# The last row of the first sweep ends in two halves of 256 columns

## The chip, the cores and the metric

The kernel runs on one core of a Trainium2 chip. The metric is the device time of one execution in microseconds. Three runs of the kernel before took 1407.41, 1408.8 and 1412.98 us; their median is 1408.8 us. The profile comes from a further execution that took 1410.98 us and whose span, from the first to the last instruction, is 1409.2 us.

## What is computed

Four graph layers follow one another over N = 4096 nodes with 64 features and one adjacency matrix `adj` of 4096 x 4096 (64 MB in f32). Each layer's result is added to its input and layer-normalised. Only the first layer matters here, a Chebyshev filter with four weights:

```
def layer0(x, L, weight):                 # L = adj, K = 4
    terms = [x, L @ x]
    for _ in range(2, K):
        terms.append(2.0 * (L @ terms[-1]) - terms[-2])
    return einsum('kni,kio->no', stack(terms), weight)
x = layernorm(x + layer0(x, adj, L0_weight))
```

The kernel works it backwards, so that features and weights are multiplied first. With w0 to w3 the four weights, b3 = x w3, b2 = x w2 + 2 A b3, b1 = x w1 + 2 A b2 - b3, and the layer gives x w0 + A b1 - b2. Three products with the whole matrix follow one another, and each needs the one before.

## The kernel before, in words

**Tiles.** The 4096 rows are 8 groups (`NG`) of 512 rows, the columns 8 groups of 512. A tile is 512 rows by 512 columns, 1 MB. `cheb_n` holds for each of 32 blocks of 128 nodes three slots of 64 features: slot 0 is b3, slot 1 becomes b2, slot 2 becomes b1. `nat_a` collects the layer's result.

**The first sweep** (the loop over `g` near line 640) loads every tile of `adj` as it stands (`raw`, SyncE's DMA queue), row group after row group, the columns from the last to the first. A tile is turned by 16 TensorE transposes (L657) into four PSUM tiles `tp`, which ScalarE copies to the turned tile `at` (L664). The turned tile is written back to memory (`adj_t`, GpSimd's queue, L686) for all that follows. VectorE takes a row sum and a minimum from the raw tile (L688, L690, 2.3 us each). The products of a tile are put one tile late: `tile_before`, the function of the previous tile, is called after the transposes of the current one. A tile at or right of the diagonal is multiplied by `halves` (L559): 64 feature columns of weights, blocks of even and odd number into the two halves of the partitions of `h_ps`. A tile left of the diagonal is multiplied by `both` (L566): slots 0 and 1 of `cheb_n` together, 128 weight columns, so that `w_ps` holds A b3 in partitions 0 to 63 and A b2 in 64 to 127 (b2 of the lower row groups is there by then).

**The end of a row** is `after_first`. VectorE adds the A b3 part of `w_ps` to `t_h`, the copied `h_ps` (L604), and ScalarE copies its A b2 part to `t_w` (L605). Then come four steps. `first` turns `t_h` back to rows and adds it twice into slot 1, which is b2 of this row (L580 or L585, then L588). `on_diagonal` multiplies the diagonal tile by that b2 into `d_ps` (L559) and adds `t_w` (L614). `second` does for slot 2 what `first` did for slot 1. `taken_off` subtracts b2 from `nat_a` on GpSimd (L622). In rows 0 to 6 these steps lie one by one between the tiles of the next row. In the last row, g = 7, nothing is left to put between, and they follow one another.

`twice_into` has two ways. Rows up to 4 use pair products: `t` is the weight and `pair`, two identity matrices of 64 stacked, the moving operand, which turns the block and adds its two halves in one product (L585). Rows 5 to 7 use transposes (L580) and two additions of 64 features each (L588, twice).

**The second sweep** goes through the tiles right of the diagonal, from row group 6 down. Its first tile is (6, 7), whose weights are slots 1 and 2 of the *last* row group (`both`, L566, target `pass`). VectorE makes the tile's mask (L754, 1.2 us) and GpSimd's queue stores it (L497). The tiles come from `adj_t` through SyncE's queue (L712), each into a buffer that a matmul or a mask of an older tile has to free first. The third sweep (L559, `pass`) follows in the same manner, and then the other layers.

**Order.** Operations recorded through `in_order` keep their program order on their engine; the others are placed by a scheduler. PSUM has eight banks: three `tp`, two `post`, and one each for `h_ps`, `w_ps` and `d_ps` (the pool `ps_a`). The targets of the second sweep use the banks of `h_ps` and `w_ps` in turn.

Of the kernel before, what the change touches and what calls it, by code (L numbers as in the profile page):

```python
# [9 lines left out]
F32 = mybir.dt.float32  # L10
# [5 lines left out]
ALU = mybir.AluOpType  # L16
# [46 lines left out]
def gnn4_kernel(  # L63
# [21 lines left out]
    nc = tc.nc  # L85
    P = 128
    N, F = x.shape
    NB = N // P
    GB = 4
    GW = GB * P  # L90
    NG = NB // GB
    CB = 4
# [26 lines left out]
    def load_raw(g, c):  # L119
        raw = row_tile("raw")  # L120
        nc.sync.dma_start(raw, adj[gcols(g), c * CB * P : (c + 1) * CB * P].rearrange("(b p) j -> p b j", p=P))
        return raw
# [19 lines left out]
    pair = const.tile([P, F], F32, name="pair")  # L142
# [25 lines left out]
    nat_a = keep.tile([P, NB, F], F32, name="nat_a")  # L168
# [36 lines left out]
    def in_order(ins):  # L205
        return tc.keep_in_program_order(ins)

    def cols(b):
        return slice(b * P, (b + 1) * P)

    def gblocks(g):
        return slice(g * GB, (g + 1) * GB)
# [312 lines left out]
    with tc.tile_pool(name="acc", bufs=1) as acc_p, tc.tile_pool(  # L525
        name="cols0", bufs=4
    ) as cols_p, tc.tile_pool(name="kept0", bufs=1) as kept_p, tc.tile_pool(name="diag0", bufs=2) as diag_p, tc.tile_pool(
        name="ps_t0", bufs=3, space=PSUM
    ) as ps_t, tc.tile_pool(name="ps_a0", bufs=1, space=PSUM) as ps_a, tc.tile_pool(
        name="ps_p0", bufs=2, space=PSUM  # L530
    ) as ps_p:

        cheb_n = acc_p.tile([P, NB, 3, F], F32, name="cheb_n")

        t_w = [acc_p.tile([P, GW], F32, name=f"t_w{q}") for q in range(2)]
# [20 lines left out]
        def halves(ps, k, rhs, jb, first, last):  # L556

            q = jb % 2
            in_order(nc.tensor.matmul(  # L559
                ps[q * F : (q + 1) * F, :], lhsT=cheb_n[:, jb, k, :], rhs=rhs,  # L560
                start=first, stop=last, skip_group_check=True,
            ))

        def both(ps, k, rhs, jb, first, last):

            in_order(nc.tensor.matmul(ps, lhsT=cheb_n[:, jb, k : k + 2, :], rhs=rhs, start=first, stop=last))  # L566

        def out_of(ps, name):
            t = acc_p.tile([P, GW], F32, name=name, tag=name if name == "t_h" else "tcol", bufs=2)
            nc.scalar.copy(t, ps)  # L570
            return t

        def new_post(w=F):
            return ps_p.tile([P, GB, w], F32, name="post", tag="post")
# [23 lines left out]
        def after_first(g, t_h, w_ps, diag_at):  # L598

            gs = gblocks(g)  # L600
            d_ps = ps_a.tile([P, GW], F32, name="d_ps")
            t_d = acc_p.tile([P, GW], F32, name="t_d", tag="tcol", bufs=2)
            if g:
                in_order(nc.vector.tensor_tensor(t_h[0:F, :], w_ps[0:F, :], t_h[0:F, :], ALU.add))  # L604
                nc.scalar.copy(t_w[g % 2][F:P, :], w_ps[F:P, :])  # L605

            def first():
                twice_into(cheb_n[:, gs, 1, :], t_h, g)

            def on_diagonal():  # L610
                for k in range(CB):
                    halves(d_ps, 1, diag_at[:, k, :], g * GB + k, k < 2, k >= 2)
                if g:
                    in_order(nc.vector.tensor_tensor(t_d, d_ps, t_w[g % 2], ALU.add))  # L614
                else:
                    nc.scalar.copy(t_d, d_ps)

            def second():
                twice_into(cheb_n[:, gs, 2, :], t_d, g)

            def taken_off():
                nc.gpsimd.tensor_tensor(nat_a[:, gs, :], nat_a[:, gs, :], cheb_n[:, gs, 1, :], ALU.subtract)  # L622

            return [first, on_diagonal, second, taken_off]


        win = ExitStack()
        win_p = win.enter_context(tc.tile_pool(name="win", bufs=1, side="right"))
        loads, weight_steps = attention_weights(win_p, ps_p)
# [6 lines left out]
        while weight_steps:  # L636
            row, c = divmod(len(aside), NCH)
# [5 lines left out]
        for g in range(NG):  # L643
            h_ps = ps_a.tile([P, GW], F32, name="h_ps")
            w_ps = ps_a.tile([P, GW], F32, name="w_ps") if g else None
            row = {}
            for c in reversed(range(NCH)):
                raw = first_raw.pop() if first_raw else load_raw(g, c)
                if g == NG - 1 and 4 <= c < g:
                    at = kept_p.tile([P, CB, GW], F32, name="at", tag="at") if c == g - 1 else before[:, c - 4]  # L650
                else:
                    at = (diag_p if c == g else cols_p).tile([P, CB, GW], F32, name="at", tag="at")
                for k in range(CB):
                    jb = c * CB + k
                    tp = ps_t.tile([P, GW], F32, name="tp", tag="tp")
                    for b in range(GB):
                        in_order(nc.tensor.transpose(tp[:, cols(b)], raw[:, b, cols(k)], ident))  # L657
                        if g * GB + b == jb:
                            scrap = sm.tile([P, P], F32, name="scrap")
                            in_order(nc.vector.scalar_tensor_tensor(  # L660
                                scrap, raw[:, b, cols(k)], 1.0, ident, ALU.mult, ALU.mult,
                                accum_out=diag[:, jb : jb + 1],
                            ))
                    nc.scalar.copy(at[:, k, :], tp)  # L664
                if steps0:
                    steps0.pop(0)()
                if tile_before:
                    tile_before()

                def tile_before(h_ps=h_ps, w_ps=w_ps, c=c, at=at, g=g, row=row):  # L670
                    for k in range(CB):
                        jb = c * CB + k
                        if c < g:
                            both(w_ps, 0, at[:, k, :], jb, c == g - 1 and k == 0, c == 0 and k == CB - 1)
                        else:
                            halves(h_ps, 0, at[:, k, :], jb, c == NCH - 1 and k < 2, c == g and k >= CB - 2)
                    if c == g:
                        row["at"] = at
                        row["t_h"] = out_of(h_ps, "t_h")
                    if c == 0:  # L680
                        steps0.extend(after_first(g, row["t_h"], w_ps, row["at"]))

                if aside:
                    for work in aside.pop(0):
                        work()
                nc.gpsimd.dma_start(adj_t[g][:, c * CB : (c + 1) * CB, :], at)  # L686

                in_order(nc.vector.tensor_reduce(dpart[:, g, c, :], raw, AX.X, ALU.add))  # L688
                n = g * NCH + c
                in_order(nc.vector.tensor_reduce(lows[:, n : n + 1], raw.rearrange("p b j -> p (b j)"), AX.X, ALU.min))  # L690
                if g == NG - 1 or (g == NG - 2 and c == g):
                    here[g, c] = at
        tile_before()
        for step in steps0:
            step()
# [12 lines left out]
        def load0(g, c, free=None):  # L708
            if (g, c) in here:
                return here[g, c]  # L710
            at = free.tile([P, CB, GW], F32, name="at", tag="at" if free in (cols_p, kept_p) else "raw") if free else row_tile("at")
            nc.sync.dma_start(at, adj_t[g][:, c * CB : (c + 1) * CB, :])  # L712
            return at
# [31 lines left out]
        for g in reversed(range(NG - 1)):  # L745
            ps = ps_a.tile([P, GW], F32, name="pass2", tag=("h_ps", "w_ps")[g % 2])
            for c in reversed(range(g + 1, NCH)):
                at = load0(g, c)
# [16 lines left out]
        due, n = [], 0  # L765
        for m, g in enumerate(third_rows):
            ps = ps_a.tile([P, GW], F32, name="pass3", tag=("h_ps", "w_ps")[m % 2])
            row = list(reversed(range(g + 1)))
            if m == 0:
                row = row[4:] + row[1:4] + row[:1]  # L770
            for c in row:
                at = load0(g, c, None if (g, c) in here else third_pools.pop(0))
# [408 lines left out]
    for signed in (False, True):  # L1181
        with cmp.Else() if signed else tc.If(all_positive > 0) as block:
            cmp = block
            with tc.tile_pool(name="cols1", bufs=3 if not signed else 2) as cols_p, tc.tile_pool(name="sign1", bufs=1) as sg, tc.tile_pool(
                name="tail1", bufs=1
            ) as tl, tc.tile_pool(name="ps_a1", bufs=1, space=PSUM) as ps_a, tc.tile_pool(
                name="ps_p1", bufs=2, space=PSUM
# [141 lines left out]
    with tc.tile_pool(name="mask2", bufs=3) as mk_p, tc.tile_pool(name="wt2", bufs=3) as wt_p, tc.tile_pool(  # L1329
        name="ps_c2", bufs=1, space=PSUM  # L1330
# [30 lines left out]
        for turn, groups in enumerate(turns_of):  # L1361
# [9 lines left out]
            for h in reversed(range(2 * NB)):  # L1371
                jb, odd = divmod(h, 2)
                c, k = divmod(jb, CB)
# [4 lines left out]
                for a in range(2):  # L1378
                    for r in range(2):
                        in_order(nc.tensor.matmul(  # L1380
                            cnt[a][r * HP : (r + 1) * HP, :], lhsT=follow, rhs=chunks[c][odd][2 * a + r][:, k, :],
                            start=(h == 2 * NB - 1), stop=True, skip_group_check=True,
# [7 lines left out]
                if odd:  # L1390
                    if turn == 0 and jb == NB - 1:
# [3 lines left out]
                        ps_a = ps_a_open.enter_context(tc.tile_pool(name="ps_a2", bufs=1, space=PSUM))  # L1395
                        acc = [ps_a.tile([P, GW], F32, name=f"acc_ps{q}") for q in range(QG)]
                    continue
                two = [
                    lambda half=half, a=a, jb=jb, wt=wt, acc=acc: gather_two(jb, half, a, wt, acc)
                    for half in (1, 0) for a in range(2)  # L1400
                ]
# [37 lines left out]
    with tc.tile_pool(name="o3", bufs=1) as op, tc.tile_pool(name="cols3", bufs=3) as cols_p, tc.tile_pool(  # L1439
        name="w3", bufs=4  # L1440
    ) as wp3, tc.tile_pool(name="el3", bufs=3) as el, tc.tile_pool(name="f3", bufs=2) as fp, tc.tile_pool(
        name="r3", bufs=2
    ) as rp, tc.tile_pool(name="ps_v3", bufs=2, space=PSUM) as ps_v, tc.tile_pool(
        name="ps_a3", bufs=2, space=PSUM
# [273 lines left out]
        n = 0  # L1718
        while n < NU + 2 or turns or gathers:
# [5 lines left out]
            if n < NU:  # L1725
                if n % 2 == 0:
                    fs[n // 2] = fp.tile([P, CB, GW], F32, name="f3")
                w, cs = ws[n][:, :, columns(n)], columns(n)
# [6 lines left out]
            if n >= 2 and n - 2 < NU:  # L1735
                m = n - 2
                t, h = divmod(m, 2)
                cm = columns(m)
                hs = slice(h * HB, (h + 1) * HB)
                f, at = fs[t][:, hs, cm], own[t][:, hs, cm]  # L1740
# [4 lines left out]
                diagonal = tiles[t][0] == tiles[t][1]  # L1745
# [82 lines left out]
```

## Time and profile before

| what | value |
|---|---|
| runs | 1407.41, 1408.8, 1412.98 us |
| the profiled execution | 1410.98 us, span 1409.2 us |
| TensorE busy | 1308.8 us (93%) |
| VectorE busy | 1051.4 us (75%) |
| ScalarE busy | 805.0 us (57%) |
| GpSimd busy | 109.9 us (8%) |
| memory traffic | 294 MB read, 85 MB written |
| last raw tile's transposes end | about 348.4 us |
| first product of the second sweep | 363.14 us |

Times inside the profile are microseconds from the span's start. TensorE's matmuls are recorded in passes: an f32 product is two records, a transpose is one. Records overlap: 512 columns start every 0.43 us and are marked 0.592 us long, so pitches are read from starts. PE is TensorE's matmul row, PEld its weight loads, DVE VectorE, ACT ScalarE, POOL GpSimd and SP SyncE; "granted clock" is the share of TensorE's full clock that it was given.

### The profile page before, as it was taken

The numbers are of one execution on the slowest core, as the hardware profiler recorded it, in microseconds if no ns is written. First come the engines' busy times: TensorE is split into PE (matmuls) and PEld (weight loads), VectorE is DVE, ScalarE is ACT, GpSimd is POOL, SyncE is SP. The second block draws the span as 40 slices with busy tenths as digits, with TensorE's granted clock in tenths as the row PEclk, the third lists the DMA queues.
The fourth block names the chain that finished last, engine by engine and source line by source line (L and its number), as shares of the span: only waits on it lengthen the run. The fifth ranks groups of instructions, "written<-read, shape, count | busy, mean of one in ns | idle before, by whom it ended". The sixth has DMA issues, their size and how long they took to land.

```text
span 1409.2 us, 18984 instructions
## 1 busy us (share of the span) xinstructions
PE 1308.8 (93%) x6766; PEld 605.2 (43%) x6766; DVE 1051.4 (75%) x2010; ACT 805.0 (57%) x1341; POOL 109.9 (8%) x191
## 2 busy tenths in 40 slices
PE   7999999999899999999999999997888898999883
PEld 5655555565344334444444323333333333333331
DVE  6699998999334257787885224356999999999996
ACT  4554444343000115654424675745989999999893
POOL 2111111101122000010111000000000000000000
PEclk9999999999999999999999999998999999999997
DMA  9999999999699999999985755534235353445320
GB/s 316 404 395 391 402 411 410 410 403 392 231 380 372 389 415 372 422 358 338 329 306 185 229 178 165 181 120 180 99 141 211 147 214 150 183 162 200 141 106 12
DMA packets 108191, 382.16 MB, mean 271 GB/s; under 512 B 20276, under 2 KB 20280, under 8 KB 76472
## 3 DMA queue, kind: packets, MB, share of 16 engines
q1 hardware_dynamic: 87096, 296.17, 56.8%
q0 software_dynamic: 12736, 76.29, 13.2%
q10 hardware_dynamic: 8256, 8.39, 1.7%
q8 instruction: 56, 0.92, 0.3%
q14 instruction: 47, 0.39, 0.1%
HBM read 294.05 MB, written 85.20 MB: 269 GB/s over the span
## 4 chain that ended last, share of the span: by engine, by line
PE 61%; ACT 15%; DVE 15%; DMA 5%; issue 3%; ACTq 0%; DVEq 0%; SPq 0%
PE pass L566 7%; PE tp L657 6%; PE w_ps L566 5%; DMA raw<-in_adj_dram 4%; PE cnt_ps L1380 4%; PE a_last L1111 4%; PE a_ps L1111 4%; PE pass L559 4%; PE acc_ps L1340 4%; PE h_ps L559 3%; PE wide_last L1102 2%; PE p_ps L1102 2%; DVE rt L1756 2%; ACT w L1731 2%; ACT rt L1732 2%
## 5 line engine op out<-in xcount | busy, mean ns | idle before, releaser
L664 ACT COPY at<-tp 128x512 f32<-128x512 f32 x248 | 127.9, 599 | 119.1 <-issue 95.9
L1385 ACT ACTIVATE wt<-cnt_ps 128x512 uint16<-128x512 f32 x210 | 116.5, 596 | 65.4 <-PE cnt_ps L1380 63.3
L688 DVE TENSOR_REDUCE dpart<-raw 128x4 f32<-128x2048 f32 x64 | 145.5, 2275 | 5.4 <-DMA raw<-in_adj_dram 5.2
L1568 PE MATMUL sums_ps<-at_d,some 128*64 128x512 f32 x288 | 146.3, 629 | 2.7 <-DVE at_d L1547 1.7
L690 DVE TENSOR_REDUCE lows<-raw 128x1 f32<-128x2048 f32 x64 | 145.5, 2274 | 0.0
L657 PE MATMUL tp<-ident,raw 128*128 128x128 f32 x1024 | 131.5, 281 | 8.3 <-DMA raw<-in_adj_dram 7.3
L657 PEld LDWEIGHTS tp<-ident,raw 128*128 128x128 f32 x1024 | 115.1, 143 | 45.6 <-issue 36.5
L1580 PE MATMUL sums_ps<-at_m,some 128*64 128x512 f32 x224 | 108.6, 606 | 0.0
L1507 PE MATMUL v_ps<-rv,tr_a 64*128 64x512 f32 (+1 forms) x288 | 82.2, 649 | 21.2 <-DVE rt L1756 20.9
L566 PE MATMUL pass<-at,cheb_n 128*128 128x512 f32 x224 | 99.2, 601 | 2.4 <-DVE cheb_n L588 1.9
L566 PE MATMUL w_ps<-at,cheb_n 128*128 128x512 f32 x208 | 93.5, 593 | 0.0
L1756 DVE SCALAR_TENSOR_TENSOR rt<-v_ps,rt 128x1024 f32<-128x1024 f32 x72 | 83.3, 1157 | 5.2 <-ACT rt L1732 4.7
L1380 PE MATMUL cnt_ps<-m,follow 128*64 128x512 fp8e4 x480 | 81.7, 391 | 4.6 <-ACT wt L1385 2.1
L1744 DVE TENSOR_TENSOR at_d<-at_d,f 128x1024 f32<-128x1024 f32 x72 | 83.4, 1158 | 0.1
L1741 DVE SCALAR_TENSOR_TENSOR f<-rt,w 128x1024 f32<-128x1024 f32 x72 | 83.3, 1160 | 0.1
L1554 DVE TENSOR_TENSOR at_m<-post,at_m 128x512 f32<-128x512 f32 x112 | 75.1, 682 | 10.1 <-PE post L1552 9.9
L1767 ACT ACTIVATE rt<-rt 128x1024 f32<-128x1024 f32 x72 | 72.1, 1005 | 11.2 <-DVE rt L1756 10.7
L1387 DVE TENSOR_SCALAR wt<-cnt_ps 128x512 uint16<-128x512 f32 x46 | 31.8, 692 | 59.0 <-PE cnt_ps L1380 59.0
L1731 ACT ACTIVATE w<-w 128x1024 f32<-128x1024 f32 x72 | 72.0, 1000 | 4.8 <-DVE w L1534 4.8
L1552 PE MATMUL post<-ident,f 128*128 128x128 f32 x448 | 68.9, 284 | 4.8 <-DVE at_m L1554 4.5
L1758 ACT ACTIVATE w<-w 128x1024 f32<-128x1024 f32 x72 | 72.4, 1006 | 0.6
L1732 ACT ACTIVATE rt<-w 128x1024 f32<-128x1024 f32 x72 | 72.4, 1005 | 0.6
(404 smaller groups left out, 2271.7 us busy)
## 6 DMA issues: line engine op xcount, KB each, us to landing
at<-adj_t SPq DMA_DIRECT2D x119, 1024.0 KB, 7.7
raw<-in_adj_dram SPq DMA_DIRECT2D x64, 1024.0 KB, 13.4
adj_t<-at POOLq DMA_DIRECT2D x62, 1024.0 KB, 8.2
at_d<-adj_t SPq DMA_DIRECT2D x36, 1024.0 KB, 4.6
at_m<-adj_t SPq DMA_DIRECT2D x28, 1024.0 KB, 6.7
m<-mask_t SPq DMA_DIRECT2D x120, 128.0 KB, 2.9
m<-mask_t SPq DMA_DIRECT2D x60, 256.0 KB, 4.2
mask_t<-mask ACTq DMA_DIRECT2D x28, 256.0 KB, 7.4
```

The source lines that it names most:

```text
L566: in_order(nc.tensor.matmul(ps, lhsT=cheb_n[:, jb, k : k + 2, :], rhs=rhs, start=first, stop=last))
L657: in_order(nc.tensor.transpose(tp[:, cols(b)], raw[:, b, cols(k)], ident))
L664: nc.scalar.copy(at[:, k, :], tp)
L688: in_order(nc.vector.tensor_reduce(dpart[:, g, c, :], raw, AX.X, ALU.add))
L690: in_order(nc.vector.tensor_reduce(lows[:, n : n + 1], raw.rearrange("p b j -> p (b j)"), AX.X, ALU.min))
L1111: in_order(nc.tensor.matmul(ps[q * F : (q + 1) * F, :], lhsT=nat_a[:, c * CB + k, 0:F], rhs=of[q if signed else 0][:, k, :], start=(c == 0 ...
L1380: in_order(nc.tensor.matmul(cnt[a][r * HP : (r + 1) * HP, :], lhsT=follow, rhs=chunks[c][odd][2 * a + r][:, k, :], start=(h == 2 * NB - 1) ...
L1385: in_order(nc.scalar.activation(wt[odd][a], cnt[a], AF.Relu, scale=-128.0))
L1568: in_order(nc.tensor.matmul(bank[0:F, :], lhsT=nat_c[:, j * CB + k, :], rhs=own[t][:, k, :], start=(i == j and k == 0), stop=(j == seq[-1] ...
L1580: in_order(nc.tensor.matmul(bank[F:P, :], lhsT=nat_c[:, above * GB + k, :], rhs=mirrored[tm][:, k, :], start=(k == 0 and above == seq[0]), ...
L1732: nc.scalar.activation(rt, w, AF.Exp, scale=0.5)
L1756: nc.vector.scalar_tensor_tensor(rt, vs[n][:, :, cs], (1.0 + V_FLOOR) * SCALE, rt, ALU.max, ALU.add)
```

## The change

For the last row, g = 7, the last tile's products and the end of the row are replaced by one function, `end_of_last`. All other rows keep `after_first`.

The parts of `w_ps` from the *other* tiles of the row are closed one tile earlier (after column group 1) and taken out by `before_last`: VectorE adds the A b3 part to `t_h`, ScalarE copies the A b2 part to `t_w`. The last tile's products go in two halves of 256 of the 512 rows of the group, each into a bank of its own (`h_ps`'s and `d_ps`'s), and VectorE adds them onto `t_h` and `t_w` (`add_last`). Half 0 is turned by pair products and added into slot 1 while half 1 is still multiplied. The diagonal tile is multiplied in two halves as well, two blocks at a time, into the banks of `h_ps` and `w_ps`, and `second` is done by pair products per half. The subtraction on GpSimd comes last.

In the changed kernel's instruction order, ScalarE's, GpSimd's and SyncE's lists are the same as before, apart from line numbers. TensorE's and VectorE's differ only between the last transposes and the first product of the second sweep: TensorE has 7 instructions more and VectorE 5 more. VectorE's mask of the second sweep's first tile, which stood between the last two additions into slot 2, stands behind both.

```
+        def before_last(g, t_h, w_ps):
+            in_order(nc.vector.tensor_tensor(t_h[0:F, :], w_ps[0:F, :], t_h[0:F, :], ALU.add))
+            nc.scalar.copy(t_w[g % 2][F:P, :], w_ps[F:P, :])
+
+        def end_of_last(g, t_h, diag_at, at):
+            HW = GW // 2
+            two = [slice(0, HW), slice(HW, GW)]
+            gs, t_w7 = gblocks(g), t_w[g % 2]
+            t_d = acc_p.tile([P, GW], F32, name="t_d", tag="tcol", bufs=2)
+            pairs, w_two, d_two = {}, {}, {}
+
+            def last_products(h, ks):
+                if h not in w_two:
+                    w_two[h] = ps_a.tile([P, GW], F32, name=("h_ps", "d_ps")[h])
+                for k in ks:
+                    in_order(nc.tensor.matmul(
+                        w_two[h][:, 0:HW], lhsT=cheb_n[:, k, 0:2, :], rhs=at[:, k, two[h]], start=(k == 0), stop=(k == CB - 1)
+                    ))
+
+            def add_last(h):
+                cs, w = two[h], w_two[h]
+                in_order(nc.vector.tensor_tensor(t_h[0:F, cs], w[0:F, 0:HW], t_h[0:F, cs], ALU.add))
+                in_order(nc.vector.tensor_tensor(t_w7[F:P, cs], w[F:P, 0:HW], t_w7[F:P, cs], ALU.add))
+
+            def paired(t, h):
+                pairs[h] = o = new_post()
+                for b in range(2):
+                    in_order(nc.tensor.matmul(o[:, b, :], lhsT=t[:, cols(2 * h + b)], rhs=pair, start=True, stop=True))
+
+            def twice_half(n, h):
+                to = cheb_n[:, g * GB + 2 * h : g * GB + 2 * h + 2, n, :]
+                in_order(nc.vector.scalar_tensor_tensor(to, pairs[h][:, 0:2, :], 2.0, to, ALU.mult, ALU.add))
+
+            def diagonal(h, ks):
+                if h not in d_two:
+                    d_two[h] = ps_a.tile([P, GW], F32, name=("h_ps", "w_ps")[h])
+                for k in ks:
+                    q = k % 2
+                    in_order(nc.tensor.matmul(
+                        d_two[h][q * F : (q + 1) * F, 0:HW], lhsT=cheb_n[:, g * GB + k, 1, :], rhs=diag_at[:, k, two[h]],
+                        start=(k < 2), stop=(k >= 2), skip_group_check=True,
+                    ))
+
+            def add_diagonal(h):
+                in_order(nc.vector.tensor_tensor(t_d[:, two[h]], d_two[h][:, 0:HW], t_w7[:, two[h]], ALU.add))
+
+            last_products(0, range(CB))
+            add_last(0)
+            last_products(1, (0, 1))
+            paired(t_h, 0)
+            twice_half(1, 0)
+            last_products(1, (2, 3))
+            add_last(1)
+            for h in range(2):
+                diagonal(h, (0, 1))
+            paired(t_h, 1)
+            twice_half(1, 1)
+            for h in range(2):
+                diagonal(h, (2, 3))
+                add_diagonal(h)
+            for h in range(2):
+                paired(t_d, h)
+                twice_half(2, h)
+            nc.gpsimd.tensor_tensor(nat_a[:, gs, :], nat_a[:, gs, :], cheb_n[:, gs, 1, :], ALU.subtract)
...
                 def tile_before(h_ps=h_ps, w_ps=w_ps, c=c, at=at, g=g, row=row):
+                    if g == NG - 1 and c == 0:
+                        before_last(g, row["t_h"], w_ps)
+                        end_of_last(g, row["t_h"], row["at"], at)
+                        return
                     for k in range(CB):
                         jb = c * CB + k
                         if c < g:
-                            both(w_ps, 0, at[:, k, :], jb, c == g - 1 and k == 0, c == 0 and k == CB - 1)
+                            both(w_ps, 0, at[:, k, :], jb, c == g - 1 and k == 0, c == (g == NG - 1) and k == CB - 1)
```

## The prediction

> **What bounds the kernel now.** I read the page first. TensorE is busy for 93% of the span and leads the chain that ended last, with 61% of it. Of its 40 slices the one from 352 to 387 us, behind the first sweep, moved 231 GB/s, its neighbours 392 and 380: something stands still there.
>
> ```profile
> PE 1308.8 (93%) x6766; PEld 605.2 (43%) x6766; DVE 1051.4 (75%) x2010; ACT 805.0 (57%) x1341; POOL 109.9 (8%) x191
> PE 61%; ACT 15%; DVE 15%; DMA 5%; issue 3%; ACTq 0%; DVEq 0%; SPq 0%
> ```
>
> Then the chain of waits in order of time, for the stretch from 340 to 380 us (start, length, what):
>
> ```profile
> 348.37 6.88 PE w_ps L566 x16
> ...
> 355.27 0.69 DVE t_h L604
> ...
> 356.01 0.67 PE post L580 x4
> ...
> 356.70 0.44 DVE cheb_n L588
> ...
> 357.16 0.43 DVE cheb_n L588
> ...
> 357.64 1.96 PE d_ps L559 x8
> ...
> 359.70 0.70 DVE t_d L614
> ...
> 360.45 0.67 PE post L580 x4
> ...
> 361.14 0.42 DVE cheb_n L588
> 361.56 0.05 DVE no_negative L706
> 361.62 1.13 DVE four L754
> 362.75 0.34 DVE cheb_n L588
> 363.09 0.04 issue
> 363.14 8.83 PE pass L566 x16
> ```
>
> The reader is to see a ladder. From 355.25 to 363.14 TensorE and VectorE take turns, nobody else does anything useful, and a mask of 1.13 us (L754), which the ladder doesn't need, stands in it. The 16 records from 348.37 are the products of the last two tiles; the last tile's eight start at 351.64. So from 351.64, where the changed code begins to differ, to the first product of the second sweep are 363.14 - 351.64 = 11.50 us.
>
> Third, TensorE's busy time and granted clock (the last number but two) in stretches of 3.41 us around this place:
>
> ```profile
> 354.13:357.54 3.41, 1.76 (x7) 0.61 (x5) 1.48 (x3) 0.58 (x1) 0.00 (x0) 1.00 1.02 432
> 357.54:360.95 3.41, 2.44 (x12) 0.90 (x12) 0.74 (x2) 0.00 (x0) 0.72 (x1) 1.00 0.47 197
> 360.96:364.37 3.41, 1.49 (x7) 0.76 (x6) 1.94 (x4) 0.00 (x0) 0.57 (x1) 1.00 0.00 0
> 364.37:367.78 3.41, 3.41 (x5) 1.35 (x4) 0.00 (x0) 0.00 (x0) 0.00 (x0) 0.50 0.20 77
> 367.79:371.20 3.41, 3.41 (x9) 1.52 (x8) 0.00 (x0) 0.58 (x1) 0.00 (x0) 1.00 0.52 161
> ```
>
> The ladder has a second price. From 364.37 to 367.78 the clock is granted at 0.50, and the second sweep's first products start every 0.85 us in place of 0.43. That costs 3.41 x 0.5 = 1.71 us. The stretch ahead of it had TensorE busy for 1.49 us.
>
> Last, who holds SyncE's loads in the second and third sweep (363 to 540 us; total, times, longest):
>
> ```profile
> SPq L712 <- PE pass L566: 51.9, 22, 5.8
> SPq L712 <- PE pass L559: 42.5, 22, 6.5
> ```
>
> The loads wait for TensorE to free buffers, and the list of TensorE's waits from 363 us to the end names no DMA at all. If TensorE is earlier, the loads are too.
>
> **The change part by part.** The instruction order tells that ScalarE, GpSimd and SyncE keep their lists, so no transfer passes another. Up to 351.64 nothing moves.
>
> *The earlier close of `w_ps`.* The sums of the other tiles are complete at about 351.80 (eighth record, start 351.21 plus 0.592). VectorE has its last minimum (L690) until 351.63 and five small operations until 352.24; then L604's addition, 0.68, runs to 352.92, and the small reciprocal (0.34) behind it to 353.2. ScalarE's copy (0.58, L605) follows by 353.6. Both lie beside half 0 of the last tile and cost nothing: cover 1.7 us of products, and without that cover 0.7 us would be paid as now.
>
> *The last tile in halves.* Eight records of 256 columns. Rows of that width (L867, `post<-whh_n`) start every 0.216 us and are 0.376 long. Half 0 thus runs from 351.64, its last record starts at 353.15 and ends at 353.53. The two halves together take the 3.44 us that the whole took.
>
> *Addition of half 0.* 64 x 256 has no row. The nearest are 64 x 512 with 0.68 (L604), 128 x 256 with 0.415 (L723), and below it 128 x 128 with 0.28 (L889). I take 0.42, since at 512 columns 64 and 128 partitions cost the same (L614 is 0.68 too); bounds 0.28 and 0.68. So `t_h` is there at 353.99 (a step from TensorE to VectorE takes 0.04, back 0.06, as 355.236 to 355.274 and 355.957 to 356.013 show). TensorE meanwhile has two products of half 1 until 354.23: no wait. The pair products of two blocks are four records; L585's start every 0.112 us, so 0.45 us at most, last end 354.79, next free slot 354.62-354.68. VectorE's addition into slot 1 is 128 x 128: 0.28, ready 355.11, beside the second pair of half 1's products (to 355.48).
>
> *First half of the diagonal.* Four products of 64 weights, in pairs beside each other: L559's pairs start every 0.43 us at 512 columns, 0.216 at 256. Two halves, two blocks each: 0.86 us, to 356.35. Under them VectorE adds half 1 onto `t_h` (355.69 to 356.11). Pair products for half 1 (0.45, last end 356.91) and the addition (0.28) come to 357.23. Here nothing covers: TensorE waits about 0.5 us, to 357.29.
>
> *Second half of the diagonal.* 357.29 to 357.93 for half 0, whose addition (128 x 256, 0.42) ends at 358.39, while half 1 is multiplied until 358.37; its addition ends at 358.83. Pair products of half 0 from 358.45 to 359.11, addition 0.28 until 359.43. Pair products of half 1 from 358.95 to 359.56, addition until 359.88.
>
> *The start of the second sweep.* The small product of L705 needs the PSUM buffer that the first addition into slot 2 frees, 359.49. Its two records pass in 0.06. The first products of `pass` need only blocks 0 and 1, so they start at 359.55, and the third waits for 359.88, which is past by then. Now VectorE's mask (1.20) stands behind both additions; the store on GpSimd's queue waits for it, and that queue's next entry comes 11 us later (363.37, 374.63).
>
> **Sum.** 359.55 - 351.64 = 7.91 us in place of 11.50: 3.6 us less. Of it, 1.1 is the mask, the rest turns that overlap. Unknown: additions at 0.68 cost 0.1 at each of two places where TensorE is just covered and 0.26 at two where it isn't; five handovers may take 0.1 more each for starts of short groups (a first pass is 0.05 longer where the array is empty, 356.013 to 356.177); together 0.9. Additions at 0.28 save 0.3. So 2.7 to 3.9 us.
>
> **The clock.** In the new order TensorE stands still only for some 0.5 us at 356.8, 0.1 at 358.4 and 0.2 at 359.4. The worst stretch of 3.41 us has it busy for about 2.6 us. Before each stretch at half clock that I looked at, TensorE was busy for 1.04 to 1.87 of 3.41 us (965.1, 1023.1, 1169.9 and 1238.2 us are four others), and 2.44 was followed by full clock. So 1.7 us more go away. The bounds are 0 and 1.7. The Trainium skill, "TensorE: Matmul & The Clock Gate", section "Why this matters for your kernels", says the clock falls after an idle gap of more than about 3 us between matmul bursts. The longest gap here is 1.92 us (361.22 to 363.14) and the clock fell all the same, so the row decides; by the page alone the fall would not be this ladder's doing, and the sum would be 3.6.
>
> I take both: 3.6 + 1.7 = 5.3 us. The profiled execution (1410.98, 1.8 of it around the span) would become 1405.7. It lay 2.2 us over the median of the runs. The fall to half clock isn't special to it: any grid of 3.41 us puts a stretch with under 1.9 us of TensorE work into 358.4 to 361.8, for nine positions in ten. So the median loses the same: 1408.8 - 5.3 = 1403.5 us.
>
> **Does it last?** From 363 us on TensorE is busy nearly all the time until 700 us and its transfers hang on it. Memory is nearly full (DMA share 0.97 to 1.0 from 377 to 540), but between 360.96 and 364.37 it stood at 0.00, so there is no backlog from ahead of the ladder.
>
> **The rivals.**
>
> *The clock falls anyway* (another place of the grid, or small pair products that count little as work). For it: TensorE's work between 354 and 359 is of narrow products. Gain 3.6 alone: 1405.2 us. Against: the 1.87 us bound.
>
> *Transfers cap the gain.* In the third sweep the loads fall behind: the load issued at 514.33 landed after 13.8 us, at 528.17, for products at 532.51, so 4.3 us ahead of its use, where one issued at 454.38 was 21.4 ahead. If the transfers kept their present times, TensorE would wait there, and 5.3 would become 4.3: 1404.5. Against: they hang on TensorE's releases.
>
> *Slower.* The clock falls inside the new chain and, because the products there are narrow, isn't given back until `pass` has run for several stretches. Every 3.41 us at half clock cost 1.7. Since 5.3 are to be lost first, it decides at 10.6 us of half clock; four stretches (13.65 us) would give 3.6 + 1.7 - 6.8, 1.5 us slower, 1410.3. For it: from 104.96 the clock stayed down for 6.83 us although TensorE was busy throughout. Against: that is the longest while TensorE had work, and the fall needs a stretch under 1.9 us busy where I count 2.6 at least.
>
> *No change to see.* A stage that doesn't hang on TensorE (the ending, bound by VectorE, 92 of the last 109 us busy) absorbs it: 1408.8. Against: all of it starts from earlier stages.
>
> *More.* The nine other stretches at half clock, all after 968 us, lie elsewhere on the grid when all is earlier; one or two fewer give 1.7 each: 1400 to 1401.8. One or two more are as likely.
>
> **How the numbers follow.** Forecast 0.55; clock falls anyway 0.17; cap 0.08; slower or more falls 0.05; absorbed 0.03; more 0.12. The runs before spread by 5.6 us. The range from 1400.0 to 1407.5 leaves out about 0.17. No change can be told from one under 0.5%, 7.0 us; so faster by that needs under 1401.8: the cases of more falls gone and the edge of the forecast, 0.15. Slower by that is over 1415.8: 0.03.
>
> **What would show it.** After the change, the first record of `pass` starts 7.9 us (7.6 to 8.8) after the last tile's first record; one wait of TensorE of about 0.5 us ahead of the diagonal's second pair; the mask behind both additions; granted clock 1.00 in the first 4 us of `pass`; and starts of the third sweep and of the later layers 5 us earlier. Wrong would be: waits of TensorE on VectorE at each turn (additions dearer than 0.42), half clock in the chain, or waits of TensorE on transfers between 500 and 540 us.

## The result and the profile after

The changed kernel takes 1403.73 us (median of 8 runs, 1401.61 to 1408.86); the kernel before, measured beside it, 1408.44 us. The ratio is 0.9965 with a 95% interval from 0.9951 to 0.9978: 4.9 us less, between 3.1 and 6.9. That is clear of no change, and it is below the 0.5% (7.0 us) from which the prediction would have told a change by one comparison. A second measurement of both (`e6_after` below) gives 0.9973 (0.9956 to 0.9991).

The profiled execution took 1408.86 us, span 1407.1 us, only 2.1 us under the one before. It isn't the changed place that is small there: this execution came to the last tile later. The last tile's first record stands at 355.05 us in place of 351.64. In the traces of this case that moment lies anywhere from 347.3 to 355.1 us, with the same instructions ahead of it. All comparisons below are therefore made from the last tile's first record onward.

The chain of waits after the change, the part around the ladder (start, length, what):

```profile
...
355.22 1.73 PE h_ps L643 x8
356.94 0.86 PE d_ps L643 x4
357.81 0.39 PE post L655 x4
358.20 0.92 PE d_ps L643 x4
359.12 0.58 PE h_ps L666 x4
359.70 0.43 PE w_ps L666 x4
360.13 0.60 PE post L655 x4
360.73 0.02 issue
360.76 0.30 DVE cheb_n L659
361.06 0.04 issue
361.10 0.68 PE h_ps L666 x4
361.78 0.02 issue
361.80 0.44 DVE t_d L672
362.24 0.04 issue
362.28 1.10 PE post L655 x8
363.39 0.13 PE low_ps L775 x2
363.51 7.07 PE pass L566 x16
...
```

The ladder has two rungs left where VectorE is on the chain, L659 and L672, in place of six and a mask. The mask is nowhere in it. By the records' starts the way from the last tile to the second sweep is 363.44 - 355.05 = 8.39 us, where it was 11.50.

TensorE's waits on VectorE (total, times, longest), in the kernel before from 350 to 364 us:

```profile
PE pass L566 <- DVE cheb_n L588: 1.9, 1, 1.9
PE d_ps L559 <- DVE cheb_n L588: 1.0, 1, 1.0
PE post L580 <- DVE t_d L614: 0.9, 1, 0.9
PE post L580 <- DVE t_h L604: 0.8, 1, 0.8
```

and in the changed kernel from 340 to 385 us:

```profile
PE pass L566 <- DVE cheb_n L792: 0.5, 1, 0.5
PE h_ps L666 <- DVE cheb_n L659: 0.4, 1, 0.4
```

The second is the wait ahead of the diagonal's second pair; the first lies inside the second sweep, between two of its rows, and the kernel before has it too (L722 there).

TensorE's busy time and granted clock (last number but two) in the new ladder and behind it:

```profile
358.82:362.23 3.41, 2.98 (x22) 1.49 (x20) 1.56 (x4) 0.00 (x0) 0.72 (x1) 1.00 1.02 430
362.23:365.64 3.41, 3.36 (x15) 2.11 (x16) 2.19 (x5) 0.00 (x0) 0.12 (x1) 1.00 0.19 74
```

The clock stays at 1.00. From the first record of `pass` to the ninth are 3.54 us, where they were 5.23.

And the holders of SyncE's loads in the second and third sweep:

```profile
SPq L782 <- PE pass L566: 48.3, 22, 3.0
SPq L782 <- PE pass L559: 41.1, 21, 6.5
```

As before, they wait for TensorE. The third sweep begins 108.94 us after the last tile's first record, where it began 113.74 us after it: 4.80 us less, 3.11 of the ladder and 1.69 of the clock.

### The profile page after: what moved, and what is told of

Its sections match the earlier page's. It is cut to its first block, busy times and chain, and to the rows that moved or that the text cites. A ratio compares the mean times of both kernels' runs of the same rounds, so it can differ in the third digit from the quotient of the medians.

```text
span 1407.1 us, 19039 instructions
## 1 busy us (share of the span) xinstructions
PE 1310.2 (93%) x6790; PEld 611.1 (43%) x6790; DVE 1052.1 (75%) x2015; ACT 805.7 (57%) x1341; POOL 110.5 (8%) x191
## 3 DMA queue, kind: packets, MB, share of 16 engines
q10 hardware_dynamic: 8256, 8.39, 1.7%
## 4 chain that ended last, share of the span: by engine, by line
PE 59%; ACT 15%; DVE 15%; DMA 6%; issue 3%; SPq 1%; ACTq 0%; POOL 0%; DVEq 0%
PE pass L566 7%; PE tp L723 6%; PE w_ps L566 6%; PE pass L559 4%; PE cnt_ps L1450 4%; PE a_last L1181 4%; PE a_ps L1181 4%; PE acc_ps L1410 3%; DMA raw<-in_adj_dram 3%; PE h_ps L559 3%; ACT w L1801 2%; ACT rt L1802 2%; DVE rt L1826 2%; ACT w L1586 2%; DVE at_m L1624 2%
## 5 line engine op out<-in xcount | busy, mean ns | idle before, releaser
L723 PE MATMUL tp<-ident,raw 128*128 128x128 f32 x1024 | 134.4, 285 | 9.8 <-DMA raw<-in_adj_dram 8.3
```

## The experiments

The table puts the traces side by side. Ladder: from the last tile's first record to the first of the second sweep. Nine: from there to the ninth record. Third: from the last tile's first record to the third sweep's first. End: from the third sweep's last record to the end of the span. All are read from the traces' records, in us. `e3_one_bank`, `e4_two_masks` and `e8_before` ran once each (1402.88, 1405.98 and 1412.99 us), so only their traces are used.

| kernel | ladder | nine | third | end | half clock behind the ladder |
|---|---|---|---|---|---|
| before | 11.50 | 5.23 | 113.74 | 873.7 | 3.41 us |
| `e8_before` | 11.50 | 5.23 | 113.75 | 875.7 | 3.41 us |
| after | 8.39 | 3.54 | 108.94 | 873.0 | none |
| `e6_after` | 8.39 | 3.54 | 108.94 | 873.8 | none |
| `e1_pairs` | 10.42 | 3.54 | 110.96 | 876.0 | none |
| `e7_pairs` | 10.42 | 3.54 | 110.97 | 874.7 | none |
| `e2_fill` | 11.49 | 3.54 | 112.04 | 873.3 | none |
| `e3_one_bank` | 9.61 | 3.54 | 110.16 | 873.3 | none |
| `e4_two_masks` | 10.37 | 5.23 | 112.62 | 872.7 | 3.41 us |
| `e5_reorder` | 7.96 | 3.54 | 108.51 | 871.7 | none |
| `e9_eight_masks` | 17.94 | 5.88 | 120.83 | 875.4 | 10.24 us, from inside the ladder on |

**Pair products alone (`e1_pairs`).**

```
         def twice_into(to, t, g):
-            if g > NG // 2:
+            if NG // 2 < g < NG - 1:
```

> The kernel before with one part of the change alone: the last row is turned back by pair products like rows 0 to 4, in whole blocks, with no halves. My theory: the first turn costs the same (eight records in place of four, 0.45 us more, one addition in place of two, 0.46 us less); in the second turn the mask and the second addition go out of the chain (1.13 + 0.34 + 0.05 us), and the pair products add 0.45. From the last tile's first record to the first product of the second sweep 10.4 us, where the kernel before has 11.50 and the changed one 8.39. The half-clock stretch behind it may stay or go (the stretch ahead would have TensorE busy for about 2.0 of 3.41 us). Total 1.1 us less than before, 2.8 if the clock holds. Rival, that the mask was no real part of the chain and the halves carry all of it: 11.5 us.

Measured: 10.42 us, 1.08 less than before. The total is 1407.87 us (10 runs), ratio 1.0 (0.9981 to 1.0018). The end of its chain of waits:

```profile
355.34 0.70 DVE t_d L614
356.04 0.04 issue
356.08 1.12 PE post L585 x8
357.20 0.02 issue
357.23 0.42 DVE cheb_n L588
357.65 0.06 DVE no_negative L706
357.71 4.55 PE pass L566 x10
```

One addition in place of two, and the mask is gone from behind it. So of the ladder's 3.11 us, 1.08 need no halves: with a single addition, the scheduler had no gap between two additions to put the mask into. The 1.08 are net, since the pair products themselves take longer than the transposes (1.12 us against 0.67). The halves bring the other 2.03. The clock held as well, so the way to the third sweep is 2.78 us shorter. The total didn't show that, which is taken up below.

**The pauses filled (`e2_fill`).**

```
+        def fill(g, at, n):
+            if g < NG - 1:
+                return
+            if "ps" not in filled:
+                filled["ps"] = ps_t.tile([P, GW], F32, name="fill", tag="tp")
+            for k in range(n):
+                in_order(nc.tensor.matmul(
+                    filled["ps"][:, 0 : GW // 2], lhsT=cheb_n[:, k, 0:2, :], rhs=at[:, k, 0 : GW // 2], start=True, stop=True
+                ))
...
+                fill(g, diag_at, 2)
                 twice_into(cheb_n[:, gs, 1, :], t_h, g)
+                fill(g, diag_at, 2)
...
+                fill(g, diag_at, 2)
                 twice_into(cheb_n[:, gs, 2, :], t_d, g)
...
         nc.vector.tensor_scalar(no_negative, low_ps, 0.5, None, ALU.is_lt)
+        fill(NG - 1, row["at"], 4)
```

> The kernel before with ten products of 256 columns added in the four pauses of the last ladder (2, 2, 2 and 4), each into a PSUM bank that nobody reads. Nothing needed is moved. The ladder's length should stay at 11.5 us (to 11.7). My theory (the clock falls after a stretch of 3.41 us with TensorE busy for under about 1.9 us): no half-clock stretch behind the ladder, the first eight records of the second sweep 0.43 us apart, 1.7 us less in all, 1406.7 against 1408.4. Rival (the fall is not this ladder's doing, since its longest pause is under 2 us): half clock as before, no gain.

Measured: the ladder is 11.49 us, and the clock stays at full. TensorE's busy time and clock in the stretches up to the second sweep's start at 360.18 and behind it:

```profile
355.00:358.41 3.41, 3.41 (x19) 1.68 (x16) 0.92 (x2) 0.00 (x0) 0.45 (x1) 1.00 0.34 142
358.41:361.82 3.41, 3.41 (x12) 2.09 (x12) 1.72 (x4) 0.00 (x0) 0.57 (x1) 1.00 0.10 35
361.82:365.20 3.38, 3.38 (x9) 1.52 (x8) 0.00 (x0) 0.58 (x1) 0.00 (x0) 1.00 0.36 84
```

Work that nobody needs, put into pauses of 0.8 to 1.9 us, makes the way to the third sweep 1.70 us shorter. At this execution's place in the grid (the falls of the clock in a trace lie on a grid of 3.413 us) the ladder without the filling would have had a stretch with 1.17 us of work, as the records of the kernel before laid on this grid show. The total is 1406.53 us against 1408.02 beside it, ratio 0.9987 (0.9973 to 1.0002): in line with 1.7, and with nothing. The trace decides: the fall belongs to this ladder, and the rival falls.

**The bank of its own taken away (`e3_one_bank`).**

```
-                        w_two[h][:, 0:HW], lhsT=cheb_n[:, k, 0:2, :], rhs=at[:, k, two[h]], start=(k == 0), stop=(k == CB - 1)
+                        w_ps[:, two[h]], lhsT=cheb_n[:, k, 0:2, :], rhs=at[:, k, two[h]],
+                        start=False, stop=(k == CB - 1), skip_group_check=True,
...
-                in_order(nc.vector.tensor_tensor(t_h[0:F, cs], w[0:F, 0:HW], t_h[0:F, cs], ALU.add))
-                in_order(nc.vector.tensor_tensor(t_w7[F:P, cs], w[F:P, 0:HW], t_w7[F:P, cs], ALU.add))
+                in_order(nc.vector.tensor_tensor(t_h[0:F, cs], w_ps[0:F, cs], t_h[0:F, cs], ALU.add))
+                in_order(nc.vector.tensor_copy(t_w7[F:P, cs], w_ps[F:P, cs]))
...
-                        before_last(g, row["t_h"], w_ps)
```

> The changed kernel without the banks of their own and without the early addition of the other tiles' sum: the last tile's two halves are added up in w_ps itself, and VectorE adds or copies half by half from that bank. The instruction order shows the first product of half 1 waiting for VectorE's two operations on half 0. My theory: TensorE then stands for 0.42 + 0.43 + 0.25 us, 1.1 us, and the way from the last tile's first record to the second sweep is 9.5 us in place of 8.39. Rival (the wait is covered later, in the pauses of the chain): 8.4 to 8.9 us. Clock at 1.00 behind it by either.

Measured: 9.61 us, 1.22 more than the changed kernel. Its chain of waits shows where:

```profile
347.73 1.74 PE w_ps L637 x8
349.47 0.02 issue
349.49 0.42 DVE t_h L644
349.91 0.01 issue
349.92 0.44 DVE t_w L645
350.36 0.04 issue
350.40 1.13 PE w_ps L637 x4
```

Half 1's products wait for both of VectorE's operations on half 0. None of it is covered later. The bank of its own, and the early sum that it needs, are 1.22 of the 2.03 us that the halves bring. The wait stands in the instruction order of this kernel; whether the chip itself would need it wasn't tried.

**Two unneeded masks in the new ladder (`e4_two_masks`).**

```
+            idle = [acc_p.tile([P, CB, GW], MASK, name="idle", tag=f"t_w{1 - g % 2}") for _ in range(2)]
+            for scrap in idle:
+                in_order(nc.vector.tensor_scalar(scrap, at, 0.0, None, ALU.not_equal, saturate=False))
             for h in range(2):
                 paired(t_d, h)
```

> The changed kernel with two more masks of 128 x 2048 (1.20 us each, results not used) on VectorE between the last addition onto t_d and the additions into slot 2. My theory: the second sweep starts 1.9 to 2.1 us later (8.39 becomes 10.4), in one pause of about 2.1 us, and for some seven places in ten of the grid of 3.41 us a stretch with under 1.9 us of TensorE work lies there, so that the clock falls to 0.50 once behind it: 3.7 us more than the changed kernel in all. Rival (the clock falls only after a pause of more than 3 us): 2.0 us more and full clock.

Measured: 10.37 us, 1.98 more, and the clock falls. The pause, and the stretches around it:

```profile
PE low_ps L778 <- DVE cheb_n L659: 1.9, 1, 1.9
```

```profile
353.69:357.10 3.41, 2.93 (x22) 1.98 (x20) 1.92 (x5) 0.00 (x0) 0.72 (x1) 1.00 0.81 341
357.10:360.51 3.41, 1.50 (x5) 0.76 (x6) 3.29 (x6) 0.00 (x0) 0.00 (x0) 1.00 0.05 14
360.52:363.93 3.41, 3.41 (x5) 1.34 (x4) 0.00 (x1) 0.00 (x0) 0.57 (x1) 0.50 0.20 77
```

A stretch with 1.50 us of work, one pause of 1.9 us in it, and half clock behind. The way to the third sweep is 112.62 us, 3.68 more than the changed kernel's, as my theory had it (3.7). So a delay of 2 us on this ladder cost 3.7 in this execution. Whether the clock falls hangs on where the ladder lies in the grid: by the records, 78% of the places would put a stretch with at most 2.02 us of work into it, 47% one with at most 1.5.

**Four steps in another order (`e5_reorder`).**

```
-            for h in range(2):
-                diagonal(h, (0, 1))
+            diagonal(0, (0, 1))
             paired(t_h, 1)
             twice_half(1, 1)
+            diagonal(1, (0, 1))
```

> The changed kernel with the order of four steps changed: half 1 of the diagonal's first two blocks is multiplied behind the pair products of half 1, so that it lies beside VectorE's addition into slot 1, where TensorE stood for 0.5 us. My theory: the pair products start 0.43 us earlier, the diagonal's second pair 0.4 us earlier, and all behind it: 8.0 us from the last tile's first record to the second sweep in place of 8.39, full clock behind it, and 0.4 us less in all, too little for the total to show. Rival (the wait only moves to the next turn): 8.4 us.

Measured: 7.96 us. In its chain of waits the first of the two rungs is gone; TensorE goes from product to product until 356.31:

```profile
354.08 0.58 PE h_ps L666 x4
354.66 0.59 PE post L655 x4
355.25 0.58 PE w_ps L666 x4
355.83 0.48 PE h_ps L666 x4
356.31 0.02 issue
356.33 0.44 DVE t_d L672
```

The wait was covered, not moved. The total is 1402.71 us (12 runs), ratio to before 0.9976 (0.9961 to 0.999); the changed kernel beside it has 0.9973. By the trace this version is 0.43 us shorter than the changed kernel up to the third sweep; the totals can't tell the two apart.

**The changed kernel once more (`e6_after`).**

> The changed kernel once more. By my theory the way from the last tile's first record to the second sweep is 8.39 us again, to the first product of the third sweep 108.9 us, with no half clock between; the total is 4.8 us (3 to 6.5) under the kernel before. Rival (the first result was helped by where the falls of the clock lay in the other stages): the same way in the trace, but a total of 0 to 2 us under the kernel before.

Measured: 8.39 and 108.94 us again, no half clock; 1404.17 us (12 runs) against 1407.95, ratio 0.9973 (0.9956 to 0.9991): 3.8 us less, 1.3 to 6.2. The rival's 0 to 2 us lie mostly outside.

**Pair products once more (`e7_pairs`).**

> Pair products alone, once more. Its trace was 2.8 us shorter up to the third sweep, its total only 0.15 us shorter with an interval of 2.6 us to both sides. Theory (the local gain stays, the total was scattered by the first sweep and by the falls of the clock in the last layers): 10.42 us again, 111.0 us to the third sweep, a total of 1 to 4 us under the kernel before. Rival (something after the third sweep gives it back): the same way up to there, and a total within 1 us of the kernel before, with a longer way from the third sweep's end to the end.

Measured: 10.42 and 110.97 us again; 1407.43 us (12 runs), ratio 0.999 (0.9967 to 1.0014), 1.4 us less with 4.6 less and 2.0 more as the ends. Alone, that holds the 2.8 us of the trace, and it holds nothing. The end took 874.7 us, between the 873.7 and 875.7 of the kernel before. The local gain is there in both traces, and neither total shows it; what the two say together is told under "What stays open".

**The kernel before once more (`e8_before`).**

> The kernel before once more, for its profile. By my theory the way to the second sweep is 11.50 us again and, for nine places in ten of the grid of 3.41 us, a half-clock stretch follows it, so that the third sweep starts 113.7 us after the last tile's first record. Rival (the fall of the clock was chance): full clock and 112.0 us.

Measured: 11.50 and 113.75 us, with the same fall:

```profile
360.58:363.99 3.41, 1.49 (x8) 0.83 (x8) 1.94 (x4) 0.00 (x0) 0.57 (x1) 1.00 0.01 2
363.99:367.40 3.41, 3.41 (x5) 1.35 (x4) 0.00 (x0) 0.00 (x0) 0.00 (x0) 0.50 0.20 77
```

**Eight unneeded masks (`e9_eight_masks`).** The edit of `e4_two_masks` with `range(8)`.

> The changed kernel with eight unneeded masks (about 1.15 us each, 9.2 together) ahead of the additions into slot 2, to see whether time lost in the ladder reaches the end of the program whole. My theory (all later work hangs on the ladder): 17.2 to 17.4 us from the last tile's first record to the second sweep, half clock for one or two stretches behind it (1.7 to 3.4 us), the third sweep 119.5 to 121.5 us after the last tile's first record, 10.5 to 12.5 us over the changed kernel's 108.94, and a total longer than the changed kernel's by the same, 1414 to 1417 us. Rival (transfers or the last layers take up part of what is lost or gained here): a total under 1411 us.

Measured: 17.94 us, above the 17.2 to 17.4 that I expected: the masks start every 1.26 us, each 0.03 us behind the end of the one before, and not every 1.15. TensorE's pause is 9.5 us. Half clock lasts three stretches, 4.8 us of it behind the second sweep's start. The third sweep starts 120.83 us after the last tile, 11.9 more than in the changed kernel, within the 10.5 to 12.5. The total is 1418.14 us (4 runs), ratio to before 1.0072 (1.0047 to 1.0098): 10.1 us over before, where the trace has 120.83 - 113.74 = 7.1 up to the third sweep and the interval goes from 6.6 to 13.8. The total ended above my 1414 to 1417: it is some 14 us over the changed kernel's medians (1403.73 and 1404.17), where the way to the third sweep is 11.9 longer and the end in the trace 1.6 to 2.4 longer. The rival's 1411 is far away. Nothing behind the ladder took up the loss.

## Why the prediction was right

*The sum.* Forecast 5.3 us, traced 4.80, timed 4.9 and 3.8. Its two terms were both there. That the first total comes within 0.1 us of the trace is luck: its interval is 3.8 us wide, and the last layers alone differ by 4 us between traces.

*The ladder* was the term that was off: 3.6 forecast, 3.11 measured, inside the bounds of 2.7 to 3.9. Up to the pair products of half 0 each start came within 0.01 us of the working: addition of half 0 begun 1.93 us after the last tile's first record, pair products at 2.59, addition into slot 1 ended at 3.47. The unknown addition of 64 x 256 took 0.415 us where 0.42 was taken. Behind that, five starts of short groups were dearer than the pitches that I used: the first product after the pair products 0.27 us in place of 0.216 (358.035 to 358.307), the switch to 64 weights 0.31 (358.739 to 359.048), the first diagonal pair 0.27, the switch to the pair products 0.31, and their first pass 0.16 in place of 0.056. Together 0.4 us by 361.05, and nothing covers them; the last turn adds the other 0.08. The prediction had named this as "five handovers may take 0.1 more each" and left it out of the middle value; the trace would have given it, since 356.013 to 356.177 and the 0.48 from 357.643 to 358.123 were such starts. The uncovered wait was 0.4 us where 0.5 was foreseen. The lower bound was added up wrongly: two times 0.1, two times 0.26 and five times 0.1 are 1.2 and not 0.9, so these unknowns reach down to 2.4 us. The measured 3.11 lies inside either.

*The mask* out of the chain: right, and `e1_pairs` prices it with the single addition that displaces it at 1.08 us. No run takes the mask alone out.

*The clock*: 1.7 forecast, 1.69 measured. That the fall follows a stretch with little work and not one long pause was argued from rows before; `e2_fill` and `e4_two_masks` have shown it from both sides. "TensorE: Matmul & The Clock Gate" of the Trainium skill, section "Why this matters for your kernels", warns of idle gaps of more than about 3 us; no gap in the ladder of the kernel before or of `e4_two_masks` was over 2 us, and the clock fell in both, so the traces decide. The bound of 1.9 us wasn't sharp: the first of the prediction's own rows has 1.76 us of work, and full clock behind it. Laid at any place of the grid, the ladder before has a stretch with at most 1.68 us of work, and at seven places in ten one with at most 1.5; the new ladder never has one under 2.9. The clock's fall was no special case of one execution either: both profiles of before have it, neither of after.

*Does it last?* Right up to where the traces can be laid on each other. From the third sweep's last record to the last product of the masks' counting (`cnt_ps`, 427.3 to 427.8 us later) all eleven traces agree within 0.6 us. Transfers didn't cap it: the load of the third sweep that was the tightest in the working landed 4.9 us ahead of its use, where it was 4.3 before. (The DMA share that the working gave as 0.97 to 1.0 fell to 0.70 and 0.84 in single stretches of 5 us, from 482 and from 382 us on; no step hung on that.) Of the rivals, that the clock falls anyway, that transfers cap, and that it is slower are refuted by the traces; that there is no change to see, by the totals. *More*, gained by fewer falls in the last layers, isn't in the totals.

*What stays open.* From there to the end the traces differ by 4 us (871.7 to 876.0), in good part with the place and number of the half-clock stretches of the last layers. One part of their work, which begins 418 us behind the third sweep's last record, shows it. Here it is in the kernel before and in `e1_pairs` (its length, and as last number but two the mean granted clock):

```profile
953.71:1007.98 54.27, 44.32 (x243) 18.22 (x240) 44.17 (x106) 37.89 (x49) 1.21 (x3) 0.87 0.39 155
946.58:1003.18 56.60, 47.41 (x243) 20.82 (x240) 44.16 (x106) 37.89 (x49) 1.22 (x3) 0.79 0.38 148
```

It took 54.3 to 54.4 us in the five traces in which the clock first falls 432.5 to 433.0 us behind the third sweep's last record (both of before are among them), 56.6 in both traces of pair products (fall at 431.9 and 432.0), and 55.2 to 55.9 in the other four (433.2 to 434.5). So the traces of pair products lose here 2.3 of the 2.8 us that they had gained. Their 22 runs taken together have a mean of 1407.3 us, the 52 of the kernel before beside them 1408.3: 1.0 less, and drawn again at random from these runs 2.5 less to 0.4 more. The 2.8 isn't in that, so the total kept less than the local gain. That the falls in the last layers are the reason is likely but not shown, since only two of the 22 have a trace. The changed kernel loses 1.4 to 1.7 us in the same part and is shorter behind it; that its total shows the whole gain is luck in part. The first sweep's length, which differs by 7.8 us, scatters the totals too; why it differs wasn't tried.

## What to carry to other kernels

A ladder of short steps between TensorE and another engine has two prices: its length, and the clock behind it, when TensorE has little work in some 3.4 us (here surely at 1.5 us and less, at times up to 2.0). Halving the work so that one half is multiplied while the other is added paid on both here, with a bank for each half; with one bank for the two, half 1 waited for the reader of half 0, and 1.22 us were lost. Look at what a scheduler has put between the steps: one mask of 1.1 us stood in this chain, and taking it out with one of two additions brought a third of what the ladder gained. And price the first product of each short group from a row of its own, not from the pitch of a long one.

## What the runs showed of the hardware

The granted clock fell to 0.50 after stretches of 3.41 us with 1.49 and 1.50 us of TensorE work and no pause over 2 us, and it didn't fall when useless products filled the same pauses. Useless work on an idle engine made the kernel's way 1.7 us shorter. I had not expected it to be that exact: 113.74 - 112.04 = 1.70.

In each of the eleven traces the changes of the clock lie on one grid of 3.413 us. Of the stretches of this grid from 20 us on that ran at full clock, all 52 with at most 1.5 us of TensorE work were followed by half clock, 40 of the 89 with 1.5 to 2.02 us, and none of the 4147 with more. In one of the stretches before a fall no pause was over 0.6 us (`e8_before`, 1347.0 to 1350.4 us, 1.96 us of work).

The way from the last tile to the third sweep, some 109 to 114 us with all its transfers, repeats to 0.01 us between executions (113.74 and 113.75, 108.94 twice, 110.96 and 110.97), while the totals of the same kernels spread by 6 us and more. For a change of this size the trace's own differences measure the changed place; whether the total keeps them is another question, as the pair products show.
